# Cross-attention and quantised feed-forward on one core: two heads in one matmul for q, k and the output projection, a new order of the first block, and a later begin of the second block's attention

## The chip, the cores and the metric

The kernel runs on one core of a Trainium2 chip, in one launch. The metric is the device time of a launch in microseconds; lower is better. The core's engines work side by side, each through its own instructions in order: TensorE (PE, with its weight loads, PEld), VectorE (DVE), ScalarE (ACT), GpSimd (POOL), and SyncE (SP), which here only issues DMAs. They wait for each other by semaphores.

## The reference, cut to what matters

`x` and `ctx` have the shape 32 x 64 x 512 (batch, D = 64 rows, L = 512), all in fp32. The projections act on the 64 rows, not on the 512 features; a head is a slice of 64 features, so there are 8.

```python
def _proj(W, b, x):                       # W is 64 x 64
    return jnp.einsum('oi,bil->bol', W, x) + b[:, None]

def attention(xn, ctx):
    q, k, v = _proj(Wq, bq, xn), _proj(Wk, bk, ctx), _proj(Wv, bv, ctx)
    # eight heads of 64 features: scores are 64 x 64 for each batch and head
    scores = jnp.einsum('hbdk,hbek->hbde', qh, kh) / 8
    p = softmax(scores, axis=-1)
    xh = jnp.einsum('hbde,hbek->hbdk', p, vh)
    return _proj(Wo, bo, xh)

x = x + attention(layernorm(x), ctx)
h = layernorm(x)
gate, up = dequantize(...), dequantize(...)   # 512 x 1792, (int - zero) * scale by groups of 128 rows
x = x + (silu(h @ gate) * (h @ up)) @ down    # down is 1792 x 512
```

## The kernel before

**Tiling.** Two batches make a pair (128 partitions: 2 x 64 rows), two pairs a set, four pairs a block (512 rows). There are 16 pairs, 8 sets, 4 blocks. For each block the kernel does attention, flips the normalised result (`flip`) into columns `hTh` and `hTl` (a high part in fp32r and the rest), and runs the feed-forward over 14 slices `f` of 128 inner features.

**Feed-forward.** `gate_up(t, f)` takes four steps `g`; each multiplies the integer weights `ng` and `nu` by the high and the low part (L597: four matmuls of 128 x 512), and ACT rescales the sums in PSUM between the groups (L607). After the last group ACT applies Silu (L610), DVE multiplies (`h`, L613), POOL splits `h` into `hh` and `hl` (L623, L624). `down(t, f)` multiplies these by `nd` (L642, L645), and DVE adds to `y` (L653). The weights come as integers; their zero points are subtracted on POOL for `ng` and `nu` (L295) and on DVE for `nd` (L301), in four chunks of up to 512 inner features (`weight_steps`). The zeros of a chunk lie in a buffer of one copy, so those of the next are loaded only when the last chunk is done with them.

**Attention.** An `Attention` object works on one pair (first block) or on a set (others); its methods are the steps. `stats`, `scale`, `apply`: layer norm on DVE and POOL. `k` and `q`: projections on PE by `heads` (L393), evacuated with the bias by DVE (`k_out`, `q_out`, L404). `v` (L427, L436). `scores` (L444), `highest`, `less`, `exp`, `sums`, `divide` (softmax on DVE, ACT and, for `divide`, POOL, L481). `turn` (L490) multiplies the weights by the output projection, so that the output comes turned for `weigh` (L506). `residual` (L518) adds to x, then a second layer norm, `flip` (L529), `high` (ACT), `low` (DVE, L543). Where two batches `b` lie on the two halves of the partitions and two heads `h` side by side, `heads` and `turn` go through a list of quarters (chunk, b, h): each matmul uses 64 rows and 64 columns of the array, with the quarter picked by b and h, and the output of batch b goes to PSUM bank b. An fp32 matmul becomes two in the machine, each with its load of weights.

**Order.** The first block's steps follow the string `START`, written out by hand, for all engines. The rest runs in rounds, 28 to a block. In each round there is one step of two lanes of `gate_up`, one step of attention for the next block, and two steps of `down` (six rounds behind), and in the first block some steps of `weight_steps`; from these a scheduler orders the instructions of each engine. The attention steps of a round are those between two bars of `ROUND_STEPS`:

```python
ROUND_STEPS = """
    0.stats 0.scale | 0.k 0.k_out | 0.v 0.v_out 0.apply | 0.q 0.q_out 1.context |
    0.scores 0.highest | 0.less 0.exp | 0.sums 0.divide | | 1.stats 1.scale |
    0.turn 0.turn_out | 0.weigh 0.residual | | 0.stats2 0.scale2 | 0.apply2 3.rows |
    ...
```

The PSUM of the attention of later blocks is one buffer of two banks, so a step that fills it waits until DVE or ACT has emptied it. `finish` (L667) uses the same buffer in rounds 7 and 11 of later blocks (`FINISH_AT`).

Of the kernel before, what the change touches and what calls it, by code (L numbers as in the profile page):

```python
# [26 lines left out]
def kernel(  # L27
# [41 lines left out]
    nc = tc.nc  # L69
    B, D, L = x.shape  # L70
    I = gate_w.shape[1]
    P = 128
    NH, HD = 8, L // 8
# [40 lines left out]
    with ExitStack() as fast:  # L114
# [4 lines left out]
        zeros = fast.enter_context(tc.tile_pool(name="zeros", bufs=1))  # L119
# [3 lines left out]
        def load_rows(j: int, pairs: list = [range(SET)]):  # L123

            xs[j] = rows.tile([P, SET, L], F32, tag="x", name=f"x_{j}", bufs=3)
            for some in pairs:
                load_pairs(xs[j], x_rows, j, some)
# [40 lines left out]
        WK, WV, WQ, WO = range(4)  # L168
# [40 lines left out]
        def proj(m: int, b: int) -> bass.AP:  # L209
            return w_T[ts(b, D), (m - b) % 4, :]  # L210
# [75 lines left out]
        def weight_steps(zs):  # L286

            for i, (at, n) in enumerate(wide):
                if i:
                    zs = load_zeros(at, n)  # L290
                z16, z8 = zs
                for g in range(KT):
                    for m, dst in enumerate((ng, nu)):
                        piece = dst[:, g, at : at + n]
                        nc.gpsimd.tensor_tensor(  # L295
                            piece, piece.bitcast(F32), z16[:, m, g, :n], ALU.subtract
                        )
                        yield
                for i in range(n // P):
                    piece = nd[:, at // P + i, :]  # L300
                    nc.vector.tensor_tensor(piece, piece.bitcast(F32), z8[:, i, :], ALU.subtract)  # L301
                    yield
# [19 lines left out]
        class Attention:  # L322
# [62 lines left out]
            stats2, scale2, apply2 = stats, scale, apply  # L385


            def heads(self, part: str, m: int, name: str):
                pp, quarters = self.quarters(name)
                src = self.by_head(part)  # L390
                with self.in_order():
                    for c, b, h in quarters:
                        nc.tensor.matmul(  # L393
                            pp[ts(h, HD), b, c, :],
                            src[ts(b, D), c, h, :],
                            proj(m, b),
                            start=True,
                            stop=True,
                        )
                return pp  # L400

            def with_bias(self, part: str, pp: bass.AP, m: int):
                b = bqk[:, m, :].unsqueeze(1).unsqueeze(1).to_broadcast([P, 2, self.n * KT, D])
                nc.vector.tensor_tensor(self.by_bank(part), pp, b, ALU.add)  # L404

            def k(self):
                self.pk = self.heads("c", WK, "pk")

            def k_out(self):
                self.with_bias("k_eT", self.pk, 1)  # L410

            def q(self):
                self.pq = self.heads("xn", WQ, "pq")

            def q_out(self):
                self.with_bias("q_e", self.pq, 0)
# [66 lines left out]


            def turn(self):
                self.pe, quarters = self.quarters("pe")
                e = self.by_head("q_e")
                with self.in_order():
                    for c, b, h in quarters:
                        nc.tensor.matmul(  # L490
                            self.pe[ts(h, D), b, c, :],
                            e[ts(b, D), c, h, :],
                            proj(WO, b),
                            start=True,
                            stop=True,
                        )

            def turn_out(self):
                nc.scalar.copy(self.by_bank("k_eT"), self.pe)
# [46 lines left out]
        def make_block(t: int):  # L546
            hTh[t] = blk.tile([P, KT, TB], F32R, tag="hTh", name=f"hTh_{t}")
            hTl[t] = blk.tile([P, KT, TB], F32R, tag="hTl", name=f"hTl_{t}")
# [3 lines left out]
        ROUND_STEPS = """  # L552
# [5 lines left out]
            1.weigh 1.residual | 1.stats2 1.scale2 | 1.apply2 4.rows | 1.flip 1.high 1.low | |  # L558
        """
        FINISH_AT = 7, 11  # L560

        def load_context(j: int):
            newest["SP"] = load_pairs(place["c"], c_rows, j, range(SET))

        def attention_steps(t: int):
            make_block(t)
            sets = {}
            for steps in ROUND_STEPS.split("|"):
                for step in steps.split():
                    i, what = int(step[0]), step[2:]  # L570
                    j = t * PB // SET + i
                    if j * SET >= NPAIR:
                        continue
                    if what == "context":
                        load_context(j)
                    elif what == "rows":
                        load_rows(j)
                    else:
                        if j not in sets:
                            sets[j] = Attention(j * SET, SET, place, two_banks)  # L580
                        getattr(sets[j], what)()
                yield
# [140 lines left out]
        def advance(steps, n: int = 1):  # L723
            for _ in range(n):
                next(steps, None)

        def chain(*gens):
# [4 lines left out]


        START = """
            0.stats 0.scale 0.apply 1.stats projections 1.scale biases 1.apply
            projections_out 2.stats 0.k biases_out 2.scale 3.stats 0.q 1.k 0.q_out
            3.scale 1.q 0.k_out zeros 2.apply 0.scores 1.q_out 2.k 0.highest 0.less
            2.k_out 0.exp 1.k_out 0.sums 2.q 3.apply 3.k 0.divide 2.q_out 3.q
            3.k_out weights 2.scores 3.q_out 0.turn 2.highest 3.scores 0.turn_out
            2.less 1.scores 3.highest 2.exp 3.v 3.less 1.highest 0.v 3.exp 1.less  # L740
            3.v_out scales 2.sums 1.v 0.v_out 1.exp 3.sums 2.v 2.divide 1.v_out
            0.weigh 1.sums 3.divide scales_out 2.v_out 0.residual 0.stats2 2.turn
            1.divide 3.turn 2.turn_out 2.weigh 3.turn_out quotients 0.scale2 1.turn
            2.residual 2.stats2 3.weigh 1.turn_out 1.weigh 1.residual 1.stats2
            2.scale2 0.apply2 1.scale2 2.apply2 0.flip 3.residual 3.stats2 2.flip
            0.high 2.high 1.apply2 3.scale2 integers integers integers integers
            0.low 1.flip 3.apply2 2.low 1.high 3.flip 1.low 3.high 3.low
        """
        place = places(att)
        with (  # L750
# [23 lines left out]
            for step in START.split():  # L774
# [4 lines left out]
                elif step == "zeros":  # L779
                    zeros_to_dram()  # L780
                    weights = weight_steps(load_zeros(*wide[0]))
# [38 lines left out]
        attend, finishing, tops = iter(()), iter(()), top_steps()  # L820
# [5 lines left out]
        with ExitStack():  # L826
            for r in range(NBLK * ROUNDS + LAG):
                t, k = divmod(r, ROUNDS)
                if k == 0:
                    attend = attention_steps(t + 1) if t + 1 < NBLK else iter(())  # L830
                if k == LAG and t > 0:
                    finishing = finish(t - 1)
                next(lanes[0], done)

                with ExitStack() as behind:
                    if r == 0:
                        behind.enter_context(tc.issue_after(newest["DVE"]))
                    advance(attend)
                if r >= LAG:
                    advance(downs)  # L840
                if r >= 2:
                    next(lanes[1], done)

                with ExitStack() as behind:
                    for ins in newest.values():
                        behind.enter_context(tc.issue_after(ins))
                    if r in (0, 5, 13):
                        load_weights(*wide[(0, 5, 13).index(r) + 1])
                    if r < ROUNDS:
                        advance(weights, 2 if r < 4 else 1 + r % 2)  # L850
                    else:
                        advance(tops, 1 + (r % 4 == 3))
                    if k in FINISH_AT or k + 2 in FINISH_AT:
                        advance(finishing)
                if r >= LAG:
                    advance(downs)
                if r == ROUNDS:
                    with tc.issue_after(newest["DVE"]):
                        last_quotients()
                if r in (BOUNDS_AT, BOUNDS_AT + 4):  # L860
                    with tc.issue_after(newest["DVE"]):
                        next(bounds, None)
# [3 lines left out]
    with tc.If(nc.values_load(flag, min_val=0, max_val=1) != 0), ExitStack() as slow:  # L866
# [20 lines left out]
        for at, n in wide:  # L887
            c = slice(at, at + n)
# [6 lines left out]
        for p in range(NPAIR):  # L895
            xp = work.tile([P, L], F32, tag="x", name=f"f_x_{p}")
            nc.sync.dma_start(xp, x1_dram[:, p, :])
            xn = work.tile([P, L], F32, tag="xn", name=f"f_xn_{p}")
# [76 lines left out]
```

## Time and profile before

| | |
|---|---|
| time, median of 3 runs (lowest to highest) | 460.54 us (457.05 to 462.57) |
| profiled execution | 457.47 us |
| its span, first to last instruction | 454.7 us |
| mean TensorE clock in it | 0.97 |
| PE matmuls | 414.0 us busy, 4175 instructions |
| DVE / ACT / POOL busy | 331.5 / 309.1 / 280.0 us |
| first feed-forward matmul begins at | 44.90 us |
| HBM read and written | 27.37 and 8.42 MB |

Sections of the page that are used below: the busy time and number of instructions of each engine; the span in 40 slices, where a digit is a share in tenths (PEclk is the clock granted to TensorE). In the views in order of time a row has its start, its length, engine, line, operation, output and inputs, rows * columns of the array for PE, shape and count; in brackets stands how long the engine was idle before, and what ended it. "issue" is time in which nothing that the profile shows was waited for. A row with a count merges instructions of the same form.

### The profile page before, as it was taken

The page shows a single profiled execution, that of the slowest core. Times are in us where ns is not written, and L with a number is a line of the kernel's source. Part 1 is how long each engine was busy: PE and PEld are TensorE (multiplying, and loading weights), DVE is VectorE, ACT ScalarE, POOL GpSimd, SP SyncE. Part 2 cuts the span into 40 slices and gives each one's busy share as a digit, 9 for nine tenths or more (in the row PEclk, how much of TensorE's full clock was granted, in tenths as well). Part 3 has the DMA queues.
Part 4 walks back from the last instruction along what each step waited for, and adds up shares of the span by engine and source line. Part 5 has one row for each costly group of instructions (what it writes and reads, how often), then busy time and mean ns, then how long its engine had stood idle before and what let it go on. Part 6 is the DMA issues. An engine that isn't in the chain of part 4 may idle for free.

```text
span 454.7 us, 10323 instructions
## 1 busy us (share of the span) xinstructions
PE 414.0 (91%) x4175; PEld 316.3 (70%) x4175; DVE 331.5 (73%) x510; ACT 309.1 (68%) x473; POOL 280.0 (62%) x293
## 2 busy tenths in 40 slices
PE   4755998998999999999999899999999999999991
PEld 4743564766677776777778577786778888887871
DVE  4878653797979983696869775586869655668673
ACT  2142589665787669686788569786688778777760
POOL 5335739658474487676787686764566887783311
PEclk9885899999999999999999999999999999999997
DMA  6793779436102020141000012130001012100004
GB/s 207 234 306 137 217 227 257 130 105 183 54 22 77 1 94 1 46 140 50 1 16 32 2 48 94 48 94 1 1 1 48 1 47 86 54 1 0 1 2 146
DMA packets 20928, 36.55 MB, mean 80 GB/s; under 512 B 1848, under 2 KB 7432, under 8 KB 20872
## 3 DMA queue, kind: packets, MB, share of 16 engines
q1 hardware_dynamic: 14056, 24.20, 16.0%
q0 software_dynamic: 6208, 11.01, 8.6%
q8 instruction: 35, 0.57, 0.5%
q10 hardware_dynamic: 608, 0.59, 0.4%
q14 instruction: 21, 0.17, 0.1%
HBM read 27.37 MB, written 8.42 MB: 79 GB/s over the span
## 4 chain that ended last, share of the span: by engine, by line
PE 43%; POOL 25%; issue 14%; DVE 10%; DMA 3%; ACT 3%; ACTq 0%; POOLq 0%; SPq 0%; DVEq 0%
PE pu L597 10%; PE pg L597 10%; POOL hl L624 7%; PE pd L642 6%; PE pd L645 5%; POOL squares L318 4%; POOL squares L316 4%; POOL hh L623 3%; DVE xn_set L112 3%; DVE y L653 2%; DMA z<-z_dram 2%; POOL q_e_set L481 2%; POOL nu L295 2%; POOL ng L295 1%; DVE k_eT_set L404 1%
## 5 line engine op out<-in xcount | busy, mean ns | idle before, releaser
L653 DVE SCALAR_TENSOR_TENSOR y<-pd,s_all,y 128x512 f32<-128x512 f32 x204 | 150.1, 743 | 47.0 <-PE pd L645 44.2
L607 ACT ACTIVATE pg<-pg,s_q 128x512 f32<-128x512 f32 x168 | 111.5, 665 | 74.2 <-PE pg L597 72.9
L607 ACT ACTIVATE pu<-pu,s_q 128x512 f32<-128x512 f32 x168 | 110.8, 660 | 4.1 <-PE pu L597 4.1
L642 PE MATMUL pd<-hh,nd 128*128 128x512 f32 x224 | 93.9, 419 | 1.6 <-DVE y L653 1.1
L597 PE MATMUL pg<-hTh,ng 128*128 128x512 f32 x224 | 91.2, 407 | 4.5 <-POOL ng L295 1.4
L623 POOL CAST hh<-h 128x512 fp32r<-128x512 f32 x55 | 35.1, 637 | 92.3 <-DVE h L613 90.7
L597 PE MATMUL pu<-hTh,nu 128*128 128x512 f32 x224 | 90.3, 403 | 0.8 <-POOL nu L295 0.5
L597 PE MATMUL pg<-hTl,ng 128*128 128x512 f32 x224 | 89.3, 399 | 0.0
L597 PE MATMUL pu<-hTl,nu 128*128 128x512 f32 x224 | 88.9, 397 | 0.0
L645 PE MATMUL pd<-hl,nd 128*128 128x512 f32 x224 | 88.7, 397 | 0.1
L624 POOL TENSOR_TENSOR hl<-h,hh 128x512 fp32r<-128x512 f32 x55 | 72.0, 1309 | 4.4
L613 DVE SCALAR_TENSOR_TENSOR h<-pu,s_all,g 128x512 f32<-128x512 f32 x56 | 41.8, 747 | 34.3 <-ACT g L610 27.8
L318 POOL TENSOR_TENSOR squares<-squares 128x512 f32<-128x512 f32 (+1 forms) x46 | 55.1, 1197 | 1.7
L597 PEld LDWEIGHTS pg<-hTh,ng 128*128 128x128 f32 x224 | 42.2, 189 | 18.3 <-ACT pg L607 3.9
L642 PEld LDWEIGHTS pd<-hh,nd 128*128 128x128 f32 x224 | 42.0, 188 | 18.0 <-DVE y L653 5.0
L597 PEld LDWEIGHTS pu<-hTh,nu 128*128 128x128 f32 x224 | 42.2, 188 | 13.9 <-ACT pu L607 2.8
L597 PEld LDWEIGHTS pu<-hTl,nu 128*128 128x128 f32 x224 | 42.2, 188 | 9.9 <-issue 0.4
L597 PEld LDWEIGHTS pg<-hTl,ng 128*128 128x128 f32 x224 | 42.4, 189 | 9.0
L610 ACT ACTIVATE g<-pg,s_all 128x512 f32<-128x512 f32 x56 | 38.8, 693 | 13.9 <-PE pg L597 12.1
L645 PEld LDWEIGHTS pd<-hl,nd 128*128 128x128 f32 x224 | 42.1, 188 | 7.9 <-POOL hl L624 0.5
L295 POOL TENSOR_TENSOR ng<-ng,z 128x512 fp32r<-128x512 f32 (+1 forms) x16 | 16.6, 1040 | 8.0 <-DMA z<-z_dram 8.0
L295 POOL TENSOR_TENSOR nu<-nu,z 128x512 fp32r<-128x512 f32 (+1 forms) x16 | 17.1, 1069 | 0.0
(290 smaller groups left out, 484.0 us busy)
## 6 DMA issues: line engine op xcount, KB each, us to landing
z<-z_dram SPq DMA_DIRECT2D x6, 512.0 KB
x<-in_x_dram SPq DMA_DIRECT2D x6, 512.0 KB
ng<-in_L_ffn_gate_w_dram POOLq DMA_DIRECT2D x3, 1024.0 KB, 5.9
nu<-in_L_ffn_up_w_dram POOLq DMA_DIRECT2D x3, 1024.0 KB, 7.7
nd<-in_L_ffn_down_w_dram POOLq DMA_DIRECT2D x3, 1024.0 KB, 10.6
c_set<-in_ctx_dram SPq DMA_DIRECT2D x6, 512.0 KB
x_dram<-x SPq DMA_DIRECT2D x6, 512.0 KB
r<-x_dram SPq DMA_DIRECT2D x6, 512.0 KB
```

The lines of the kernel that those rows point to most:

```text
L295: nc.gpsimd.tensor_tensor(piece, piece.bitcast(F32), z16[:, m, g, :n], ALU.subtract)
L316: nc.gpsimd.tensor_tensor(square[:, :n], piece, piece, ALU.mult)
L318: nc.gpsimd.tensor_tensor(total[:, :n], total[:, :n], square[:, :n], ALU.add)
L597: nc.tensor.matmul(acc, w[:, g, ts(f, P)], half[:, g, :], start=(g == 0 and half is hi), stop=(g == KT - 1 and half is lo), skip_group_che ...
L607: nc.scalar.activation(acc, acc, AF.Copy, scale=by)
L610: nc.scalar.activation(g_sb, acc, AF.Silu, scale=by)
L613: ins = nc.vector.scalar_tensor_tensor(h_sb, acc, by, g_sb, ALU.mult, ALU.mult)
L623: nc.gpsimd.tensor_copy(hh, h_sb)
L624: ins = nc.gpsimd.tensor_tensor(hl, h_sb, hh.bitcast(F32), ALU.subtract)
L642: nc.tensor.matmul(pd, w, h_hi[t, f], start=(t, f) != LAST, stop=False, skip_group_check=True)
L645: nc.tensor.matmul(pd, w, h_lo[t, f], start=False, stop=True, skip_group_check=True)
L653: ins = nc.vector.scalar_tensor_tensor(y, pd, by, y, ALU.mult, ALU.add)
```

## The change

`heads` is replaced by `within`, which `k`, `q` and now `turn` call too. It makes one matmul for a chunk and batch where there were two: the two heads of the chunk become 128 columns of the array on the 64 rows of the batch. The outputs land where they did. The string `START` has another order: `v` stands ahead in each pair, pair 0 goes through to its flip early, the second pair's rows and the last pair's follow otherwise. The attention of the second block starts in the fourth round (`FIRST_AT = 3`) and for that block the two empty rounds 7 and 11 of `ROUND_STEPS` are skipped.

```diff
-            def heads(self, part: str, m: int, name: str):
+            def within(self, part: str, m: int, name: str):
                 pp, quarters = self.quarters(name)
                 src = self.by_head(part)
                 with self.in_order():
-                    for c, b, h in quarters:
-                        nc.tensor.matmul(
-                            pp[ts(h, HD), b, c, :],
-                            src[ts(b, D), c, h, :],
-                            proj(m, b),
-                            start=True,
-                            stop=True,
-                        )
+                    for c, b in [q[:2] for q in quarters[::2]]:
+                        two = src[ts(b, D), c, :, :].rearrange("p h d -> p (h d)")
+                        nc.tensor.matmul(pp[:, b, c, :], two, proj(m, b), start=True, stop=True)
                 return pp
...
             def k(self):
-                self.pk = self.heads("c", WK, "pk")
+                self.pk = self.within("c", WK, "pk")
...
             def q(self):
-                self.pq = self.heads("xn", WQ, "pq")
+                self.pq = self.within("xn", WQ, "pq")
...
             def turn(self):
-                self.pe, quarters = self.quarters("pe")
-                e = self.by_head("q_e")
-                with self.in_order():
-                    for c, b, h in quarters:
-                        nc.tensor.matmul(
...
-                        )
+                self.pe = self.within("q_e", WO, "pe")
...
+        FIRST_AT = 3
...
-            for steps in ROUND_STEPS.split("|"):
+            for k, steps in enumerate(ROUND_STEPS.split("|")):
+                if t == 1 and k in FINISH_AT:
+                    continue
...
         START = """
-            0.stats 0.scale 0.apply 1.stats projections 1.scale biases 1.apply
-            projections_out 2.stats 0.k biases_out 2.scale 3.stats 0.q 1.k 0.q_out
-            3.scale 1.q 0.k_out zeros 2.apply 0.scores 1.q_out 2.k 0.highest 0.less
-            2.k_out 0.exp 1.k_out 0.sums 2.q 3.apply 3.k 0.divide 2.q_out 3.q
-            3.k_out weights 2.scores 3.q_out 0.turn 2.highest 3.scores 0.turn_out
-            2.less 1.scores 3.highest 2.exp 3.v 3.less 1.highest 0.v 3.exp 1.less
-            3.v_out scales 2.sums 1.v 0.v_out 1.exp 3.sums 2.v 2.divide 1.v_out
-            0.weigh 1.sums 3.divide scales_out 2.v_out 0.residual 0.stats2 2.turn
-            1.divide 3.turn 2.turn_out 2.weigh 3.turn_out quotients 0.scale2 1.turn
-            2.residual 2.stats2 3.weigh 1.turn_out 1.weigh 1.residual 1.stats2
-            2.scale2 0.apply2 1.scale2 2.apply2 0.flip 3.residual 3.stats2 2.flip
-            0.high 2.high 1.apply2 3.scale2 integers integers integers integers
-            0.low 1.flip 3.apply2 2.low 1.high 3.flip 1.low 3.high 3.low
+            0.stats 0.scale 0.apply 1.stats projections 1.scale biases
+            projections_out 1.apply 2.stats 0.q biases_out 2.scale 3.stats 0.k 3.k
+            0.k_out 3.scale 0.v 0.q_out zeros 2.apply 0.scores 0.v_out 3.k_out 2.k
+            0.highest 2.q 0.less 1.k 2.k_out 0.exp 1.q 2.q_out 0.sums 1.v 2.scores
+            1.q_out 1.v_out 0.divide 1.k_out weights 2.highest 1.scores 2.less
+            3.apply 2.exp 0.turn 1.highest 3.q 1.less 0.turn_out 2.sums 2.v 1.exp
+            0.weigh 3.q_out 2.v_out 2.divide 1.sums scales 3.scores scales_out
+            0.residual 0.stats2 1.divide 2.turn 3.highest 0.scale2 3.less 1.turn
+            2.turn_out 0.apply2 3.exp 3.v quotients 1.turn_out 2.weigh 3.v_out
+            3.sums 0.flip 2.residual 2.stats2 3.divide 1.weigh 0.high 3.turn 0.low
+            2.scale2 3.turn_out 1.residual 1.stats2 3.weigh 2.apply2 3.residual
+            3.stats2 2.flip 1.scale2 2.high 1.apply2 3.scale2 integers integers
+            integers integers 2.low 1.flip 3.apply2 1.high 3.flip 1.low 3.high 3.low
         """
...
                 with ExitStack() as behind:
-                    if r == 0:
+                    if r == FIRST_AT:
                         behind.enter_context(tc.issue_after(newest["DVE"]))
-                    advance(attend)
+                    if r >= FIRST_AT:
+                        advance(attend)
```

## The prediction

> **What bounds the kernel now.** I read the page first, then a table by stretches, then TensorE's own order of time, then POOL's and the chain of waits at the start.
>
> ```profile
> span 454.7 us, 10323 instructions
> PE 414.0 (91%) x4175; PEld 316.3 (70%) x4175; DVE 331.5 (73%) x510; ACT 309.1 (68%) x473; POOL 280.0 (62%) x293
> ...
> PEclk9885899999999999999999999999999999999997
> ```
>
> TensorE (PE) is busy 91% of the span, and its clock is low only in the first tenth. The same by stretch (start to first feed-forward matmul, the stretch up to 86 us, the rest with attention, the rest without):
>
> ```profile
> 0.00:44.90 44.90, 25.45 (x701) 21.85 (x702) 32.87 (x72) 11.92 (x22) 19.22 (x34) 0.82 0.70 222
> 44.90:86.00 41.10, 37.47 (x434) 23.97 (x435) 22.78 (x34) 30.41 (x45) 29.87 (x30) 0.95 0.69 202
> 86.00:345.00 259.00, 250.87 (x2590) 190.61 (x2589) 203.72 (x299) 190.68 (x285) 167.42 (x169) 1.00 0.18 56
> 345.00:454.70 109.70, 100.25 (x452) 79.90 (x450) 72.12 (x109) 76.04 (x122) 63.45 (x61) 0.97 0.10 35
> ```
>
> The columns are PE, PE weight loads, DVE, ACT, POOL, then clock. From 86 us on PE is full: work added to or taken from it there moves the end one for one. In the first stretch DVE has the most work (32.9 of 44.9) and PE waits. In the second PE looks full, but overlapping records hide holes; POOL paces it (below).
>
> One step of attention for a set of two pairs, inside the full stretch:
>
> ```profile
> 160.50 0.39 PE L597 MATMUL pu<-hTh,nu 128*128 128x512 f32 x1
> 160.73 0.40 PE L597 MATMUL pu<-hTl,nu 128*128 128x512 f32 x1
> 161.06 1.02 PEld L393 LDWEIGHTS pq_8to<-w_T,xn_set 64*64 64x64 f32 x64 [0.37 <-issue]
> 161.06 1.16 PE L393 MATMUL pq_8to<-w_T,xn_set 64*64 64x64 f32 x64
> 162.15 0.19 PEld L642 LDWEIGHTS pd<-hh,nd 128*128 128x128 f32 x1
> 162.26 0.19 PEld L645 LDWEIGHTS pd<-hl,nd 128*128 128x128 f32 x1
> ```
>
> A feed-forward matmul follows the last at 0.23 us. The q step takes 1.09 us from its first load (161.06) to the next feed-forward load (162.15). Its 64 loads go in 16 groups of four, one for each 64x64 quarter of the array: (1.02 - 0.13 for one load - 0.02 for the spread inside a group) / 15 = 0.058 us per group. And this is what a load costs: at 162.15 the first load of 128 columns after the switch is followed by the second 0.11 us later[...].
>
> ```profile
> 7.73 0.97 PEld L199 LDWEIGHTS pb<-ones,b_nat 1*128 1x128 f32 x4
> ```
>
> Here four fp32 loads of 128 columns serve matmuls of a single column, so streaming costs nothing; each still lasts 328 ns in its group's row, and the starts are (0.97 - 0.33) / 3 = 0.21 us apart, at half clock. At full clock that is 0.11 again.
>
> [...]
>
> **Part 1, two heads in one matmul.** Each of k, q and turn issues half as many matmuls and loads, each 128 columns wide on 64 rows. Streamed columns: before, four quarters at once, 64 columns each, 16 groups; after, two row halves at once, again 16 groups. So no streaming is saved. But each group now waits for a load of 128 columns, 0.11 us, where the 64 streamed columns hide 0.058. Step after: 0.11 for the first load, 15 x 0.11, then 0.15 from the last matmul to the next load as now (1.09 - 0.06 - 15 x 0.058): 1.91 us against 1.09, so +0.82. There are 3 such steps in each of 6 sets: 18 x 0.82 = 14.8 us. Bounds for the step: nothing (+0.05) if the load hides after all; +2.6 if the loads of the two row halves don't run side by side (32 x 0.11 + 0.15 = 3.67). I take +0.82, because loads of the two row halves do run together in the 64x64 mode. Numbers of k_out, q_out, turn_out on DVE and ACT stay as they are; their inputs come 0.8 later.
>
> **Part 2, new order of the first block.** Same operations; v moves ahead of the scores, pair 0 is carried through early. Now there is one long hole:
>
> ```profile
> 28.15 0.47 PE po L506 x32
> 28.62 0.28 PE pe L490 x10
> 28.90 3.48 issue
> 32.38 0.81 PE pe L490 x13
> ...
> 44.80 0.67 DVE st_4to L368 x2
> ```
>
> PE stands 3.48 us with nothing to wait for; some 1,220 PE instructions have run[...], and the weights' 3 MB are in flight. [...] The change issues 12 x 16 = 192 matmuls and 192 loads fewer in the first block[...]. Against that, 12 steps are load-bound: about +0.85 us each for the three at half clock (8 groups at 0.21 against 0.107), +0.4 for the nine others. Walking the changed order with the durations of this trace (DVE 0.69 for bias, max, less, 0.88 for sums, 0.88 for residual, 1.1 for stats, 0.55 for apply; POOL divide 1.04): the first scores end at about 16 instead of 13.3 us, DVE then has hardly a hole, the last low ends at 43.9 instead of 44.8. Gain 0.9; between -2 (more loads in the way) and 3.4 (loads hidden).
>
> **Part 3, attention of block 1 from round 3.** It moves stats, scale, k and v out of the first rounds; the two empty rounds 7 and 11 are skipped, so it still ends in round 27, one round later. What it moves on POOL:
>
> ```profile
> 47.54 0.70 POOL L374 TENSOR_TENSOR rs_4to<-rs_4to,nhalf 128x2 f32<-128x2 f32 x1 [2.01 <-DVE rs_4to L370]
> ...
> 63.78 1.16 POOL L295 TENSOR_TENSOR ng<-ng,z 128x512 fp32r<-128x512 f32 x1 [7.95 <-DMA z<-z_dram]
> 64.88 0.61 POOL L623 CAST hh<-h 128x512 fp32r<-128x512 f32 x1
> ...
> 83.90 1.16 POOL L295 TENSOR_TENSOR nu<-nu,z 128x512 fp32r<-128x512 f32 x1
> ```
>
> The second chunk's zeros can only be loaded into their buffer when POOL has used the first chunk's; eight subtracts at 1.12 us. Rs_4to stands among them, 2.01 waiting and 0.70 working. Behind them come the load (55.2 to 63.8, 8.6 us) and the second chunk's subtracts, and f = 4 needs the last of these, done at 85.1. Moving rs_4to saves 2.7; hh_0 and hl_0 now stand ahead of the wait for the zeros instead of behind it, 1.9. The divide, DMA issues (3 x 0.76) and casts behind the wait stay. On SP the same loads stand ahead of the zeros. With 0.9 from part 2 the last subtract ends near 80.5 instead of 85.1. PE's own work up to that point is 106 matmuls x 0.23 + 10 us of attention steps at their new price + 2 us at half clock from 43.9, also near 80.5; two limits this close cost about 1, so 81.5 against 85.8, where before 104 matmuls and one step more (po, 1.29) were done: 4.3 - 0.8 = 3.5 us gained, with three of the 18 dearer steps inside.
>
> At the round 27 to 28 border the flip of the second set now has some 14 matmuls (3.3 us) behind it before its low half is used, and high and low take 1.0 + 1.2: I put 0.2 of wait there.
>
> **Sum.** Profiled execution 457.47 (span 454.7, 2.8 around it). 457.5 - 3.5 + 15 x 0.82 + 0.2 = 466.5. The profiled run lies 3.1 under the median 460.54 of the runs shown; on the median's scale 469.6, which I round to 469.
>
> **Rivals.**
> - *The loads hide.* If a group of 128-column loads fits into 0.06 us, part 1 costs 18 x 0.05 = 0.9, part 2 gains 3.4, and the POOL chain ends at 78 (one for the wait: 79): 457.5 - 6.7 + 0.8 + 0.9 + 0.2 = 452.7, 455.8 on the median's scale. For it: transposes of 128 columns run at that pace[...]. It decides below about 0.08 us a group: (6.7 - 0.8) / 18 steps = 0.33 a step, over 15 groups 0.022 more than 0.058. Against it: 0.11 between full-size loads, 0.21 at half clock.
> - *The row halves load one after the other.* +2.6 a step: 457.5 + 18 x 2.6 - 2 = 502, 505 on the median's scale. Against it: the 64x64 mode.
> - *Load-bound, but the start gives more back* (hole gone and clock warm before the feed-forward): 4 us more off, 462.5, 465.6 on the median's scale: inside the likeliest case's own range, 462 to 477.
>
> **How the numbers follow.** Load-bound 0.58, hidden 0.32, one after the other 0.10. A measurement here tells about 1% (4.6 us) from no change. Load-bound: 0.50 slower, 0.06 within, 0.02 faster. Hidden, centred on -1.0% and open downwards: 0.20 faster, 0.12 within. The third: slower. Together 0.22, 0.18, 0.60. The range takes in the hidden case except its far end: 452 to 480.
>
> **What would show it.** After: a q step of a later set from first load to the next feed-forward load near 1.9 us with 32 loads (1.1: hidden; 3.7: one after the other); weight loads in that step about 0.11 apart per row half; no 3.5 us of issue near 29 us; first feed-forward matmul near 44; the first wait of POOL for zeros starting near 52 instead of 55; last second-chunk subtract near 81. The prediction is wrong if the later q steps stay at 1.1, or if the first block ends much earlier than 43 in spite of dear loads.

## The result and the profile after

The changed kernel takes 479.67 us (median of 4 runs, 476.80 to 483.41), the kernel before 459.42 beside it (457.05 to 462.57): ratio 1.0444, 95% interval 1.0399 to 1.0490, some 20 us slower. The forecast was 469.0, slower by 8.5. Its main cost, the dearer steps of the later blocks, was right in kind and size; the first block and the delay, booked together as a gain, lost.

The page of the kernel after (profiled execution 483.41 us), the rows that answer to those of before:

```profile
span 481.0 us, 8790 instructions
PE 446.7 (93%) x3407; PEld 350.5 (73%) x3407; DVE 337.0 (70%) x510; ACT 310.6 (65%) x473; POOL 281.0 (58%) x293
...
PEclk9998787999999899999999999999999999999997
```

There are 768 matmuls and as many loads fewer (4175 - 3407), and yet 33 us more of PE time. The stretches of the kernel after, cut like those of before (start to first feed-forward matmul, to 95 us, the rest with attention, the rest without):

```profile
0.00:50.51 50.51, 39.04 (x510) 34.28 (x510) 33.50 (x72) 12.47 (x22) 19.11 (x34) 0.94 0.60 193
50.51:95.00 44.49, 39.38 (x265) 29.65 (x266) 27.52 (x34) 29.68 (x43) 26.95 (x28) 0.84 0.65 191
95.00:375.00 280.00, 271.92 (x2205) 209.86 (x2205) 207.25 (x304) 195.47 (x291) 173.55 (x175) 0.99 0.16 51
375.00:481.00 106.00, 96.36 (x432) 76.69 (x430) 68.75 (x103) 72.96 (x118) 61.44 (x59) 0.97 0.11 36
```

The columns are those of before: PE, PE weight loads, DVE, ACT, POOL, clock. The first stretch is 5.6 us longer (50.51 against 44.90). DVE works as much in it as before (33.5 against 32.9), but PE is busy 39.0 instead of 25.5. In the second the clock stands at 0.84.

A q step inside the full stretch, matmuls and then loads:

```profile
178.76 0.40 PE L588 MATMUL pu<-hTl,nu 128*128 128x512 f32 x1
179.09 2.00 PE L395 MATMUL pq_8to<-w_T,xn_set 64*128 64x64 f32 x32
181.02 0.50 PE L633 MATMUL pd<-hh,nd 128*128 128x512 f32 x1
```

```profile
179.08 1.86 PEld L395 LDWEIGHTS pq_8to<-w_T,xn_set 64*128 64x128 f32 x32 [0.36 <-issue]
181.02 0.19 PEld L633 LDWEIGHTS pd<-hh,nd 128*128 128x128 f32 x1
```

From first load to next feed-forward load: 181.02 - 179.08 = 1.94 us, against 1.09 before and 1.91 predicted. The loads of the step (32 records, two for each of its 16 fp32 matmuls) are (1.86 - 0.19) / 15 = 0.111 us apart per group of two: a load of 128 columns each time, the row halves side by side.

What was not expected is the first block. TensorE in order of time, kernel after:

```profile
8.97 1.97 PE L395 MATMUL pq<-w_T,xn_set 64*128 64x64 f32 x16
10.74 3.62 PE L395 MATMUL pk<-w_T,c_set 64*128 64x64 f32 x32
14.29 1.13 PE L425 MATMUL pv<-c_set,w_T 64*64 64x256 f32 x8
15.20 1.08 PE L442 MATMUL pss<-k_eT_set,q_e_set 64*64 64x64 f32 x32
...
32.01 1.13 PE L442 MATMUL pss<-k_eT_set,q_e_set 64*64 64x64 f32 x32
33.06 3.68 PE L395 MATMUL pe<-w_T,q_e_set 64*128 64x64 f32 x32
...
50.51 0.77 PE L588 MATMUL pg<-hTh,ng 128*128 128x512 f32 x1 [1.45 <-POOL ng L295]
```

Between 8.97 and 40.69 no matmul of attention has a wait in brackets: PE is now the bound of the first block. A step of 16 matmuls takes 1.7 to 1.8 us ((14.29 - 10.74) / 2), 0.21 us per group, which is the price at half clock (the 128-column loads at 7.73 in the trace of before are 0.21 apart too). And it stays so: the unchanged pss step of 32 matmuls lasts 1.08 at 15.20 and still 1.13 at 32.01; it is 0.64 to 0.69 at full clock (below, at 14.67). The trace's clock records have the clock up first at 41.2 us; before it was 14.7, and it did not stay up there either (half clock from 18.1 to 21.6 and from 31.8 to 48.9). (PEclk shows 9 ahead of the first record, whatever the clock was. The length of a known step tells.)

The second surprise lies between 70 and 80 us. POOL, VectorE and TensorE of the kernel after there:

```profile
70.66 0.72 POOL L374 TENSOR_TENSOR rs_4to<-rs_4to,nhalf 128x2 f32<-128x2 f32 x1 [1.37 <-DVE rs_4to L370]
71.36 1.16 POOL L295 TENSOR_TENSOR ng<-ng,z 128x512 fp32r<-128x512 f32 x1
...
74.61 0.82 POOL L268 DMA_DIRECT2D ng<-in_L_ffn_gate_w_dram  x1
75.43 0.75 POOL L269 DMA_DIRECT2D nu<-in_L_ffn_up_w_dram  x1
76.16 0.76 POOL L270 DMA_DIRECT2D nd<-in_L_ffn_down_w_dram  x1
76.92 1.19 POOL L295 TENSOR_TENSOR nu<-nu,z 128x512 fp32r<-128x512 f32 x1
78.04 1.17 POOL L295 TENSOR_TENSOR ng<-ng,z 128x512 fp32r<-128x512 f32 x1
...
96.90 1.16 POOL L295 TENSOR_TENSOR nu<-nu,z 128x512 fp32r<-128x512 f32 x1
```

```profile
70.42 0.15 DVE L370 TENSOR_SCALAR rs_4to<-mv_4to 128x2 f32<-128x2 f32 x1
...
74.99 4.25 DVE L370 TENSOR_SCALAR rs_6to<-mv_6to 128x2 f32<-128x2 f32 x1
75.98 3.26 DVE L402 TENSOR_TENSOR q_e_set<-pq_4to,bias 128x1024 f32<-128x1024 f32 x1
77.11 2.12 DVE L604 SCALAR_TENSOR_TENSOR h<-pu,s_all,g 128x512 f32<-128x512 f32 x1
```

```profile
79.31 1.99 PE L442 MATMUL pss_4to<-k_eT_set,q_e_set 64*64 64x64 f32 x64 [2.54 <-DVE h L604]
81.23 0.79 PE L588 MATMUL pg<-hTh,ng 128*128 128x512 f32 x1
```

An add of two numbers per partition lasts 4.25 us on VectorE (its like, rs_4to, takes 0.15) and ends at 79.24, when POOL's subtract of 78.04 ends (79.21). The q bias and `h` behind it start about 1 us apart, but all three records end at 79.23 or 79.24. So what the trace shows held is the end of all three; the bias, 1.19 us long when nothing holds it (below, at 67.29), can't have begun only at 79.24. TensorE's scores wait 2.54 us for that end, and then run at half clock (1.99 us for 64 matmuls). Rs_4to still stands just ahead of the second chunk's first subtract, and the chunk's last subtract ends at 98.1, not at 80.5.

Where the 26 us between the two profiled executions lie: 5.6 up to the first feed-forward matmul; 16.9 in the intervals between feed-forward matmuls that hold attention (15.8 of it in those of the 18 dearer k, q and turn steps; from each interval 0.2335 us is taken off for the feed-forward matmul itself, and the trace of before is subtracted from that of after); 3.6 between feed-forward matmuls, where three half-clock spells stand (61.7 to 65.1, 78.7 to 85.6, 160.7 to 164.1). This pair is wide: the execution after lies 3.7 us above its kernel's median, and by medians the difference is 20.

### The profile page after: what moved, and what is told of

Same layout as the page of the kernel before. It is cut to its first block, busy times and chain, and to the rows that moved or that the text cites. A ratio compares the mean times of both kernels' runs of the same rounds, so it can differ in the third digit from the quotient of the medians.

```text
span 481.0 us, 8790 instructions
## 1 busy us (share of the span) xinstructions
PE 446.7 (93%) x3407; PEld 350.5 (73%) x3407; DVE 337.0 (70%) x510; ACT 310.6 (65%) x473; POOL 281.0 (58%) x293
## 4 chain that ended last, share of the span: by engine, by line
PE 45%; POOL 19%; issue 14%; DVE 10%; ACT 0%; POOLq 0%; DVEq 0%
PE pu L588 11%; PE pg L588 11%; PE pd L633 7%; PE pd L636 5%; POOL hl L615 5%; POOL squares L318 4%; DVE y L644 4%; POOL squares L316 3%; POOL hh L614 3%; DVE xn_set L112 2%; DVE h L604 1%; POOL nu L295 1%; PE pe_12to L395 1%; PE pe_8to L395 1%; PE py L658 1%
## 5 line engine op out<-in xcount | busy, mean ns | idle before, releaser
L588 PE MATMUL pg<-hTh,ng 128*128 128x512 f32 x224 | 92.2, 412 | 1.4 <-POOL ng L295 1.4
L588 PE MATMUL pu<-hTl,nu 128*128 128x512 f32 x224 | 90.4, 403 | 0.0
L636 PE MATMUL pd<-hl,nd 128*128 128x512 f32 x224 | 89.7, 401 | 0.6 <-POOL hl L615 0.6
L604 DVE SCALAR_TENSOR_TENSOR h<-pu,s_all,g 128x512 f32<-128x512 f32 x56 | 43.1, 770 | 31.2 <-ACT g L601 25.6
L588 PEld LDWEIGHTS pg<-hTh,ng 128*128 128x128 f32 x224 | 43.2, 193 | 14.2 <-POOL ng L295 1.8
L601 ACT ACTIVATE g<-pg,s_all 128x512 f32<-128x512 f32 x56 | 38.6, 690 | 16.6 <-PE pg L588 14.7
```

The source lines that it names most:

```text
L588: nc.tensor.matmul(acc, w[:, g, ts(f, P)], half[:, g, :], start=(g == 0 and half is hi), stop=(g == KT - 1 and half is lo), skip_group_che ...
L601: nc.scalar.activation(g_sb, acc, AF.Silu, scale=by)
L604: ins = nc.vector.scalar_tensor_tensor(h_sb, acc, by, g_sb, ALU.mult, ALU.mult)
L636: nc.tensor.matmul(pd, w, h_lo[t, f], start=False, stop=True, skip_group_check=True)
```

## The experiments

Each ran beside the kernel before, and its ratio is to that; the interval behind a ratio is the 95% one. Differences in time between kernels are worked out from the ratios, times 459.4 us. Theory "cold array": the dear steps of the first block stream data through TensorE only half of the time (an estimate: a group of quarters, 64 columns each, went in 0.058 us; a group of two-head matmuls, 64 columns each, takes 0.111), which doesn't bring the clock up; half clock doubles the price of their loads (0.21 us against 0.111), and so the clock stays down. Rival "order": the new order and the delayed attention lose the start by themselves.

**Which part, where?** Four kernels from the changed one or the one before.

*New order and delay, with quarters:*

```diff
-                self.pk = self.within("c", WK, "pk")
+                self.pk = self.heads("c", WK, "pk")
...
-                self.pe = self.within("q_e", WO, "pe")
+                self.pe, quarters = self.quarters("pe")
+                e = self.by_head("q_e")
...
```

> The changed kernel with k, q and turn back in 64x64 quarters, so the new order of the first block and the later start of block 1's attention alone. Theory 'cold array' (the start is lost because 12 steps bound by 128-column loads keep TensorE at half clock): clock up within the first 20 us, first feed-forward matmul at 43 to 46 us, time 453 to 461, at or under the kernel before. Theory 'order' (the new order and the delay lose the start by themselves): first feed-forward matmul near 50 us, time 466 to 470.

Measured: 462.77 us, ratio 1.0078 (1.0051 to 1.0105); clock up at 12.6, first feed-forward matmul at 43.57. Each theory is right by half: the clock comes up early and the first block recovers, yet the kernel is 3.6 us slower than before. Something after 44 us loses.

*Two heads in one matmul alone, old order, no delay:* the reverse edits on the kernel before.

> The kernel before with two heads in one matmul, old order and old start of block 1's attention. Cold array: the first block goes at half clock and its matmuls set its end, first feed-forward matmul at 49 us or later, time 478 to 484: the whole loss and a little more. Order: only the 18 later steps at about +0.76 and some first-block steps, first feed-forward matmul at 45 to 46, time 472 to 475.

Measured: 480.77, ratio 1.0468 (1.0438 to 1.0498); clock up at 29.6, first feed-forward matmul at 47.83 (a little earlier than expected). Part 1 alone, without the new order and the delay, loses as much as the whole change (the intervals overlap).

*Two heads in one matmul only in later blocks, and only in the first:*

```diff
-                self.pk = self.within("c", WK, "pk")
+                self.pk = (self.within if self.n == 2 else self.heads)("c", WK, "pk")
```

(the same for q and turn; `self.n == 1` in the second kernel)

> The changed kernel with quarters in the first block only; two heads in one matmul in the later blocks. Cold array: first feed-forward matmul back at 43 to 46 us, time that of quarters everywhere plus 18 x 0.76 = 13.7, so 467 to 474, and 6 to 12 us under the changed kernel. Order: first feed-forward matmul stays near 50, time 477 to 480.

Measured: 476.59, ratio 1.0383 (1.0349 to 1.0417), first feed-forward matmul at 44.62, clock up at 13.6. The start recovers as the cold array has it, the time only by 2.8 us: it stays above the 467 to 474 expected. Over quarters everywhere it is (1.0383 - 1.0078) x 459.4 = 14.0 us, the price of the 18 later steps: 0.78 each.

> The changed kernel with two heads in one matmul in the first block only; quarters in the later blocks. Cold array: first feed-forward matmul at 50 us as in the changed kernel, half clock up to about 41 us, time 18 x 0.76 = 13.7 under the changed kernel, so 464 to 468, and 6 to 12 us over quarters everywhere. Order: the same 464 to 468, but within 2 us of quarters everywhere.

Measured: 467.25, ratio 1.0170 (1.0140 to 1.0200); clock up only at 56.0, first feed-forward matmul at 52.14. By ratio it is 4.2 us over quarters everywhere: more than "order" allows (2), less than "cold array" expected (6 to 12). Against the changed kernel it puts the later steps at 12.6 us, where the pair above gave 14.0. The two profiled executions differ by 11 (472.11, the longest of its kernel's five, against 461.12), 8.6 of it at the first feed-forward matmul. So in the new order and with the delay the first block's dear steps cost 2.8 to 4.2 us; what the profiled executions show more was not followed up. In the old order without the delay they cost more: 480.77 is 21.5 us over the kernel before, 7.5 more than the later steps' 14.0, although no add is held up there (rs_6to takes 0.16 us). Of these, 2.9 stand at the first feed-forward matmul (47.83 against 44.90). The clock is at half again from 39.9 to 60.3, where before it is up at 48.9; an estimate of what that costs is another 4 us, half of the 8.5 us by which the half clock lasts longer behind the first feed-forward matmul. So the causes below do not simply add from every starting point.

A single profiled execution places the first feed-forward matmul only roughly: over the five kernels here with the first block of before it lies between 44.26 and 46.87, over the five with the new order and quarters between 43.32 and 44.89. The clock is the steadier sign. It comes up first between 11.4 and 14.7 us in all twelve kernels whose first block has quarters or doubled streams, and at 29.6, 41.2 and 56.0 in the three with plain two-head matmuls there.

**Is it the streaming?** The changed kernel, with each two-head matmul of the first block streaming its 64 columns twice:

```diff
+                        if self.n == 1:
+                            w = proj(m, b).unsqueeze(1).to_broadcast([D, 2, D])
+                            nc.tensor.matmul(pp[:, b, c : c + 2, :], two, w, start=True, stop=True)
+                            continue
```

> The changed kernel, but in the first block each of the 192 two-head matmuls streams its 64 columns twice (128 columns for the same 128-column load; the second copy goes to columns that the next matmul overwrites). More work, same loads. Cold array (half clock because TensorE streams only half of the time): a step at half clock still takes 1.7 us, but the array now streams all of it, so the clock comes up within the first 20 us, steps fall to about 0.95 us, the first feed-forward matmul is at 44 to 47 us and the time 474 to 478, under the changed kernel in spite of twice the streaming. Rival (the half clock comes from something else, such as the low number of instructions, the rows in use or the waits): clock up no earlier than 30 us, first feed-forward matmul at 50 or later, time 480 to 486.

Measured: 476.65, ratio 1.0346 (1.0289 to 1.0404), 4.5 us under the changed kernel's 1.0444. TensorE of this kernel in order of time:

```profile
8.57 2.08 PE L400 MATMUL pq<-w_T,xn_set 64*128 64x128 f32 x16
10.44 3.62 PE L400 MATMUL pk<-w_T,c_set 64*128 64x128 f32 x32
13.99 0.85 PE L432 MATMUL pv<-c_set,w_T 64*64 64x256 f32 x8
14.67 0.64 PE L449 MATMUL pss<-k_eT_set,q_e_set 64*64 64x64 f32 x32
15.23 1.16 PE L400 MATMUL pk<-w_T,c_set 64*128 64x128 f32 x16
16.23 1.06 PE L400 MATMUL pq<-w_T,xn_set 64*128 64x128 f32 x16
17.12 1.06 PE L400 MATMUL pk<-w_T,c_set 64*128 64x128 f32 x16
...
43.07 0.77 PE L595 MATMUL pg<-hTh,ng 128*128 128x512 f32 x1 [1.45 <-POOL ng L295]
```

The two k steps take 3.55 us as before (13.99 - 10.44): twice the streaming is free at half clock, so the loads were the bound. Then the clock comes up, at 14.4 us by its records, and a step takes 0.89 (17.12 - 16.23), about half of the changed kernel's 1.7, with twice its streaming. The first feed-forward matmul is 7.4 us earlier (in a second kernel with the same first block, the last one below, 4.2 us: 46.26, clock up at 14.6). Order, loads, number of instructions and array mode are those of the changed kernel; only the streamed columns differ. The profile's busy share could not have told. The stretch from 8 to 42 us, of the kernel after and then of the one with quarters, new order and delay:

```profile
8.00:42.00 34.00, 34.00 (x461) 30.80 (x460) 23.72 (x50) 8.08 (x15) 9.57 (x14) 1.00 0.62 195
```

```profile
8.00:42.00 34.00, 23.62 (x694) 19.98 (x693) 29.45 (x63) 9.72 (x17) 13.12 (x18) 0.77 0.72 228
```

PE is busy 34.00 of 34.00 us with a clock column of 1.00 (the first record comes at 41.2), at half clock in truth; 23.62 busy and 0.77 in the kernel whose clock had come up.

The clock changes in steps: the stretches between two changes are multiples of 3.41 us (before: 3.41, 3.41, 10.24, 17.07 and 399.36; after, the first six: 3.41, 10.24, 6.83, 3.41, 13.65 and 6.83). A TensorE that its records show busy throughout, 34.00 of 34.00 us, did not bring it up in the changed kernel before 41.2.

**Order or delay?** Each alone on the kernel before. First the new START, as in the change:

> The kernel before with the new order of the first block alone: quarters, block 1's attention from round 0. The prediction's walk put the first feed-forward matmul 0.9 us earlier; with quarters, order and delay together it was at 43.57 against 44.90, and yet that kernel was 3.4 us slower. If the delay loses it: 457 to 459.5, the same or faster than the kernel before. If the order loses it (what it leaves to POOL and DVE after the first block): 462 to 464.

Measured: 458.04, ratio 0.9957 (0.9937 to 0.9977). The new order gains 2.0 us. Where is not shown: in its profiled execution the first feed-forward matmul stands at 44.89, as before (44.90), though over the five profiled executions of each order with quarters it comes 1.1 us earlier on average (44.18 against 45.25). Then the delay (with the two rounds skipped):

```diff
+        FIRST_AT = 3
...
-                    advance(attend)
+                    if r >= FIRST_AT:
+                        advance(attend)
```

> The kernel before with block 1's attention from round 3 alone: quarters, old order of the first block. The prediction put about 2.7 us of gain here (rs_4to off POOL's chain ahead of the zeros). If the delay loses: 462 to 465, first feed-forward matmul unchanged near 44.9, with new waits between 45 and 100 us. If the order loses: 457 to 460.

Measured: 464.36, ratio 1.0094 (1.0062 to 1.0125). The delay loses 4.3 us. VectorE and TensorE of this kernel:

```profile
69.67 4.26 DVE L370 TENSOR_SCALAR rs_6to<-mv_6to 128x2 f32<-128x2 f32 x1
70.67 3.26 DVE L405 TENSOR_TENSOR q_e_set<-pq_4to,bias 128x1024 f32<-128x1024 f32 x1
```

```profile
74.00 1.46 PE L445 MATMUL pss_4to<-k_eT_set,q_e_set 64*64 64x64 f32 x64 [3.21 <-DVE h L617]
...
91.52 0.62 PE L601 MATMUL pu<-hTh,nu 128*128 128x512 f32 x1 [1.60 <-POOL nu L295]
```

The same blocked add as in the changed kernel, and a second wait, for the last subtract of the second chunk, which now stands behind block 1's first divide. The clock is at half right after both (74.7 to 78.1 and 91.8 to 95.2).

**Which of the two waits?** Theory "blocked add", rival "late subtracts"; one edit for each, then both. The first moves both adds of this set to POOL; the later one, of the second layer norm, lasted 0.16 us on VectorE, so it is the early one that counts.

```diff
-                nc.vector.tensor_scalar(self.rs, self.mv[:, :, 1], EPS, None, ALU.add)
+                add = nc.gpsimd if (self.p, n) == (6, SET) else nc.vector
+                add.tensor_scalar(self.rs, self.mv[:, :, 1], EPS, None, ALU.add)
```

> Attention from round 3 alone, as in the run with the delay alone (which measured 464.36 and showed an add of 128x2 elements on VectorE, rs_6to, lasting 4.26 us beside POOL's subtracts and DMA issues, and TensorE waiting 3.2 us for the q_e_set queued behind it). Edit: this one add is done by POOL. Theory 'blocked add' (VectorE waits for POOL's stretch of work, and block 1's scores with it): the 3.2 us wait ahead of pss_4to falls under 1 us and the time to 460.5 to 463. Rival 'late subtracts' (what costs is that POOL takes the divide ahead of the second chunk's last subtract): no change, 463.5 to 465.5.

Measured: 459.74, ratio 1.0002 (0.9979 to 1.0025): all of the delay's loss gone, more than expected. VectorE and TensorE of this kernel:

```profile
67.08 0.29 DVE L369 BATCH_NORM_AGGREGATE mv_6to<-st_6to 128x2 f32<-128x6 f32 x2
67.29 1.19 DVE L406 TENSOR_TENSOR q_e_set<-pq_4to,bias 128x1024 f32<-128x1024 f32 x1
```

```profile
68.53 1.16 PE L446 MATMUL pss_4to<-k_eT_set,q_e_set 64*64 64x64 f32 x64
```

```profile
83.47 1.15 POOL L295 TENSOR_TENSOR nu<-nu,z 128x512 fp32r<-128x512 f32 x1
```

The bias takes 1.19 instead of 3.26, and pss_4to has no wait. The last subtract, still behind the divide, ends at 84.6 instead of 91.5 (2.6 us of this because the first block of this execution ended earlier, 44.26 against 46.87), since the divide's sums come earlier: the late subtract was largely a consequence of the add.

```diff
-                        advance(weights, 2 if r < 4 else 1 + r % 2)
+                        advance(weights, 2 if r < 9 else 1 + r % 2)
```

> Attention from round 3 alone, with two of POOL's zero subtracts issued in each of the rounds 0 to 8 instead of 0 to 3 and then one or two: the second chunk's last subtract then stands ahead of the first divide of block 1 instead of behind it. Late subtracts: the last subtract of the second chunk ends near 82 instead of 91.5, the 1.6 us wait of TensorE near 91.5 goes, time 460.5 to 463. Blocked add: no change, 463.5 to 465.5, the wait ahead of pss_4to stays at 3 us.

Measured: 460.17, ratio 1.0022 (1.0000 to 1.0045), the time of "late subtracts". But it doesn't decide between the two: POOL's new sequence put rs_6to ahead of its long stretch (0.41 us instead of 4.26), and the wait ahead of pss_4to fell to 0.5.

> Attention from round 3 alone, with both edits: the add on POOL and the subtracts earlier. If the two waits (with the half-clock spells behind them) are the cost of the delay, it is gone: 457.5 to 461. If something else in the delay costs (two empty rounds skipped, block 1's flips later): 463 or more.

Measured: 461.05, ratio 1.0041 (1.0018 to 1.0064). Nothing on top: either edit takes the one loss away. It lies slightly above either alone, with intervals that still overlap; whether that is real is open.

> The kernel before with the new order of the first block (which alone measured 458.04, 0.43% under the kernel before) and POOL's subtracts two a round up to round 8; quarters, attention from round 0. If POOL's subtracts pace TensorE up to 86 us, as the prediction read it: 455 to 457.5. If they don't: 457.5 to 459.

Measured: 457.60, ratio 0.9962 (0.9944 to 0.9980), the same as the order alone (0.9957), though the second chunk's last subtract ends at 83.5 instead of 86.3. POOL's subtracts don't pace TensorE up to 86 us as the prediction read it.

**Do the causes add up?** The add on POOL goes, first, into the kernel with quarters, new order and delay; then into the one with doubled streams.

> Quarters everywhere, new order, attention from round 3 (that kernel measured 462.77, 0.78% over the kernel before), with the one add of rs_6to on POOL. If the blocked add is the whole cost of the delay in this order too: 457 to 459.5, the same as the new order alone (458.04). If the delay, freed of it, gains what the prediction put there: under 456.5. If the delay has a cost of its own beside the add: 461 to 463.

Measured: 456.77, ratio 0.9949 (0.9932 to 0.9966), the lowest median of all, below both kernels. It falls between the two ranges set for it, and its interval overlaps that of the order alone (0.9957): freed of the add, the delay neither gains nor costs anything that shows.

> The changed kernel with two repairs, each of which leaves the two-head matmuls in: in the first block every one streams its columns twice (that kernel measured 476.65), and the add of rs_6to is on POOL. If cold array, blocked add and load-bound later steps are the whole account: the kernel before plus 18 x 0.76 = 13.7, minus 2.0 for the new order, so 470 to 473.5. If something else of the loss is left, or if the add was hidden here: 475 to 478.

Measured: 471.52, ratio 1.0268 (1.0226 to 1.0310), inside the range set from the three causes: 13.7 - 2.0 = 11.7 over the kernel before (12.0 with the 14.0 measured above), 12.3 measured. What remains is the price of the later loads, less the order's gain. The blocked add has now been taken out of three kernels: it cost 4.2 us with the delay alone ((1.0094 - 1.0002) x 459.4), 5.9 with quarters, new order and delay, 3.6 with doubled streams (this last with an interval of some 3 us to each side).

## Why the prediction was right and wrong

The step that failed is the gain booked for the first block and the delay, and in it above all part 3. The 3.5 us of gain hold three dear steps as a loss (3 x 0.82) and 0.9 of part 2, so the delay was priced at a gain of 5.1. Alone it lost 4.3, on top of the new order 5.6 ((1.0078 - 0.9957) x 459.4). With the 4.3 this is 9.4 of the 11.4 us that lie between the 9.0 forecast (466.5 - 457.5) and the 20.4 measured. Two things stood in the gain's place. An add on VectorE, held up beside POOL's work, cost what the delay lost (4.2 of 4.3); the working did not contain this wait. And freed of it the delay gained nothing (0.9949 against 0.9957 for the order alone), which agrees with the run in which POOL's subtracts, which the delay was to bring forward, ended 2.8 us earlier and the time stayed (0.9962 against 0.9957). The clock of the first block, in part 2, failed too, but for less.

- **Right: part 1's mechanism and price.** Loads of 128 columns bind (0.111 us per group), the row halves load side by side, 1.94 us a step where 1.91 was written. "15 x 0.82" and the three steps booked into the start make 14.8; the 18 later steps cost 14.0 (12.6 by the other pair of kernels). The two rivals on the loads (hidden, one after the other) are out; the transposes that spoke for the first show two 64x128 loads of before 0.11 us apart (at 6.94, 0.29 us together where one lasts 0.18), just ahead of the loads at 7.73 that are 0.21 apart, the pace of the two-head loads at half clock.
- **Wrong: "about +0.85 us each for the three at half clock, +0.4 for the nine others" (part 2).** All but the last one ran at half clock, at 1.7 to 1.8 us each. The step took the clock's course from the trace of before, where it is first up at 14.7 us; but the dear steps themselves keep it down (first up at 41.2; with quarters at 12.6). Instead of a first feed-forward matmul at 43.9 it came at 50.5 in the profiled execution; in time this costs 2.8 to 4.2 us in the new order with the delay, 4.5 by the doubled streams.
- **Half right: the new order.** Alone it gains 2.0 us. The walk has the first block end at 43.9 with the dear steps in it; with quarters instead it ends between 43.32 and 44.89, so the number was met only by kernels for which it was not worked out.
- **Not borne out: that fewer instructions take away the 3.48 us hole.** It is gone in the changed kernel, as forecast. But with the same 192 matmuls fewer and the clock up (at 14.6), the last kernel has such a hole again:

```profile
25.91 0.48 PE L401 MATMUL pe<-w_T,q_e_set 64*128 64x128 f32 x3
29.08 3.36 PE L401 MATMUL pe<-w_T,q_e_set 64*128 64x128 f32 x29 [2.68 <-issue]
```

  The kernel with doubled streams, with the same first block and the clock up as well, has none; all ten kernels with quarters in the first block have one, the longest of each 1.9 to 4.2 us. Neither the number of instructions nor the clock alone tells when a hole appears; the cause was not shown.
- **Wrong: "moving rs_4to saves 2.7; hh_0 and hl_0 now ahead of the wait save 1.9" (part 3).** The sum of the last subtract is itself 0.9 short: 85.1 less 2.7, 1.9 and 0.9 is 79.6, not 80.5. What happened weighs more. Rs_4to went from ahead of the first chunk's last subtracts to just ahead of the second chunk's first. And hh_0, moved forward, waits for its own input (h_0 on VectorE from 66.44 for 0.75 us; hh_0 starts at 67.31): the first subtract of the second chunk starts at 71.4, 20.9 us after the first feed-forward matmul, before 18.9. The delay loses 4.3 us where a gain was booked, by an add on another engine that the list of moved POOL work did not hold. What was left out was in the trace of before: moving stats and scale into POOL's stretch of three DMA issues and subtracts was never priced on VectorE, although before's own rs_6to (2.01 us) stood beside such subtracts.
- **The sum.** Start and delay: order -2.0, delay +4.3, first block's loads +2.8, that is +5.1 instead of -6.0 (the -3.5 without its three later steps). Later steps +14.0. Together 19.1 of the 20.4 measured. The 2.8 and 14.0 are steps of one chain of kernels that ends at the changed one, so what the sum tests is only whether order and delay apart (+2.3) give the two together (+3.6): the 1.3 left is within the intervals of the ratios. The kernel with two repairs is the independent test. The rival in which "the start gives more back" went the opposite way.

## What to carry to other kernels

A step's price depends on the clock, and the clock on what the steps stream: when an edit makes a long stretch of matmuls at the start of a kernel bound by its weight loads, price that stretch at half clock too, and do not carry over the clock of the old trace. (Here such a step of 16 took 1.7 to 1.8 us at half clock, and 0.89 where it streamed its columns twice and the clock was up. Among feed-forward matmuls the steps of 32 ran at full clock, 1.94 us.) Fewer matmuls is no saving where loads of twice the columns take the place of streams that hid them (1.94 us against 1.09 for half the matmuls). When work is moved in time, lay it beside the other engine's work in its new place: a small VectorE operation next to a long stretch of POOL's can hold up the engine that waits for VectorE (an add of 4.25 us instead of 0.15, and 2.54 us of waiting on TensorE). And do not take a start from one profiled execution: between the changed kernel and the one with quarters in the first block it differs by 5.9 us in the profiled pair (50.51 against 44.62), and the times of the runs differ by 2.8.

## What the runs showed of the hardware

- TensorE with an unbroken row of matmuls and loads stayed at half clock for 32 us (to 41.2), and in the kernel with two heads in one matmul in the first block only to 56.0; streaming twice the columns per load brought it up at 14.4 and, in the second such kernel, 14.6. How much streaming it takes was not measured.
- The 128-column fp32 loads in the 64-row mode set a pace of 0.111 us per group at full clock and of 0.21 to 0.22 at half, with 64 columns streamed for each ((1.86 - 0.19) / 15 and 3.55 / 16) and with 128 (0.89 / 8 and 3.55 / 16).
- A 128x2 add on VectorE took 4.25 us beside POOL's DMA issues and subtracts, 0.15 to 0.33 in the other eleven of its kind in the changed kernel (up to 2.01 in the kernel before, there too beside subtracts). The wait went on over several POOL instructions in a row (from 74.99 to the end of the subtract at 79.21), and two VectorE instructions behind the add started meanwhile (75.98 and 77.11) and ended with it (79.24 and 79.23). That taking this add off VectorE removes the wait is shown (with the delay alone, the bias behind it fell from 3.26 to 1.19 us and the 3.21 us of wait on TensorE went); what holds the add was not shown.
